# A transformer block in fp32: V by Strassen products kept in DRAM, and part of the softmax's work moved from VectorE to GpSimd

## The chip, the cores and the metric

The kernel runs on one core of a Trainium2 chip. The metric is the device time of one execution in microseconds (us). Five engines matter: PE (TensorE, matrix products into PSUM), DVE (VectorE), ACT (ScalarE), POOL (GpSimd) and SP (SyncE, whose queue issues all the DMAs here). Each engine runs its own instructions in order and waits on semaphores for what others produce.

## The reference

```
x = x + layernorm(attention(layernorm(x)))
x = x + layernorm(ffn(layernorm(x)))

attention(h):                      # h is [2, 512, 512]: 2 batches of 512 tokens
    q = rms_norm(h @ Wq + bq, gq)  # Wq, Wk, Wv: [512, 4096]; the norm is over all 4096
    k = rms_norm(h @ Wk + bk, gk)
    v = h @ Wv + bv
    split q, k, v into 32 heads of 128
    attn = softmax(q @ k.T / sqrt(128)) ; out = attn @ v, heads side by side
    return out @ Wo + bo           # Wo: [4096, 512]
ffn(x): x @ W_base.T + b_base + a small gated mixture of 8 rank-16 experts
```

All is fp32. In the trace a matmul of a 128x128 by a 128x512 tile is two PE records.

## The kernel before, in words

Everything is laid in tiles of 128 partitions by 512 fp32 (256 KB). `norm_transposed` (L132) gives the normed input transposed: for each batch four tiles `nT` of 128 features by 512 tokens.

**Projections of q and k** (`project`, L173). For each of 8 groups of 4 heads a block of weights (1 MB) is loaded, and q, then k, is made by Strassen's scheme in Winograd's form over 2x2 blocks: the two halves of the features, two halves of the group's heads, and the two batches. `token_sums` (L150) forms the four sums `t1` to `t4` of the token side once, on DVE; `weight_sums` (L162) the four of the weights for each group, on GpSimd. A group is seven products of two tiles each; ACT and DVE combine them out of PSUM. `keep_it` (L204) stores each finished head to DRAM (`keptq`, `keptk`), squares it on ACT, and adds the square to `accq` or `acck` on GpSimd (L213), for the rms norms: `rqs` (for q, one value per token in every row) and `rks` (for k, one per token in a column).

**The head loop** (L434) has 64 turns, one for each head and batch (i = 2h + b). A turn's instructions are issued in the order written, since the scheduler is told to keep the order on PE, DVE, ACT and POOL (L575):

- `fetch(i+3)`: DMAs of k and q of one head back from DRAM; `scaled(i+2)` (L323): q times the gain `gqk` and times `rqs`, on DVE.
- `sums(i)` (L345): three adds on DVE, `d`, of the four exponential tiles of turn i.
- `scores(i+1)` (L329): four products `pss`, copied by ACT with the factor `rks` into a wide tile `s` of 128x2048; the maximum of the four parts on DVE (`m`), and over partitions on GpSimd with `partition_all_reduce` (`top`, L342).
- `outward`: products `psy` of a finished group's heads with Wo, added to `ys` on DVE (`y`, L405), and `values` (L304): products `psv` of V for a later group, plain products of four feature tiles, copied by ACT into SBUF.
- `turned(i)` (L354): a 32x32-block transpose `dT` and a reduction `part` on DVE, the column sums of `d`.
- `exponentials(i+1)` (L374): the maximum subtracted from all of `s` on DVE (L376), the exponential on ACT (L377).
- `weighted(i)`: four products `o` of V with the exponentials; `reciprocals(i)`: `psd` on PE spreads the sums, then `inv` and `r` on DVE; `divided(i)`: `oh` = `o` times `r` on DVE and the bias of V on ACT.

V of a group is made during the loop, one or two tiles a turn, as tables written out by hand say (`v_tasks`, `o_tasks`, L410 to L423). After the loop come the last group's `psy`, the residual, the second norm and the FFN.

Of the kernel before, what the change touches and what calls it, by code (L numbers as in the profile page):

```python
# [15 lines left out]
P = 128  # L16
# [15 lines left out]
def kernel(ctx: ExitStack, tc: tile.TileContext, x, wq, wk, wv, wo, vecs, rows, wbase, gates, bexp, out):  # L32
# [7 lines left out]


    nc = tc.nc
    B = x.shape[0]
# [7 lines left out]
    kpool = ctx.enter_context(tc.tile_pool(name="kpool", bufs=5))  # L51
    opool = ctx.enter_context(tc.tile_pool(name="opool", bufs=GH * B + 10))
    spool = ctx.enter_context(tc.tile_pool(name="spool", bufs=3))
# [9 lines left out]
    def wide(name):  # L63
        return spool.tile([P, NT, 512], F32, tag="wide", name=name)
# [38 lines left out]
    nbthr = const.tile([P, 1], F32, tag="nbthr", name="nbthr")  # L103
    gate_sb = const.tile([P, NK, E * R + E + 1], F32, tag="gate", name="gate_sb")
    nc.sync.dma_start(out=gate_sb, in_=gates.rearrange("(c p) f -> p c f", p=P))
    bexp_sb = const.tile([P, D], F32, tag="bexp", name="bexp_sb")
    nc.sync.dma_start(out=bexp_sb, in_=bexp)

# [41 lines left out]
    def token_sums(xTs):  # L150

        (b11, b21), (b12, b22) = ((xT[0:2], xT[2:4]) for xT in xTs)
        first, second = wide("t12"), wide("t34")
        t1, t2, t3, t4 = first[:, 0:2], first[:, 2:4], second[:, 0:2], second[:, 2:4]
        for c in range(2):
            nc.vector.tensor_tensor(t1[:, c], b12[c], b11[c], ALU.subtract)
            nc.vector.tensor_tensor(t2[:, c], b22[c], t1[:, c], ALU.subtract)  # L157
            nc.vector.tensor_tensor(t3[:, c], b22[c], b12[c], ALU.subtract)
            nc.vector.tensor_tensor(t4[:, c], b21[c], t2[:, c], ALU.subtract)
        return [[t[:, c] for c in range(2)] for t in (t1, t2, t3, t4)]  # L160

# [10 lines left out]

    def project(xTs, sums, w_src, bias, step, name, pool, keep, accs, w):  # L173

# [8 lines left out]
        for g in range(G):  # L183
# [20 lines left out]
            def keep_it(o, b, j):  # L204
                h = g * GH + j
                nc.sync.dma_start(out=keep[b, h], in_=o)
                if b not in begun:
                    begun.add(b)
                    nc.scalar.activation(accs[b], o, AF.Square)
                else:  # L210
                    sq = tt(f"sq_{name}{b}_{h}")
                    nc.scalar.activation(sq, o, AF.Square)  # L212
                    nc.gpsimd.tensor_tensor(accs[b], accs[b], sq, ALU.add)  # L213

            two = range(2)
# [39 lines left out]
    def attention():  # L255
# [12 lines left out]
        keptk = dram.tile([B, H, P, 512], F32, tag="k", name="keptk")  # L268
        accq = [xpool.tile([P, 512], F32, tag="x", name=f"accq{b}") for b in range(B)]
        acck = [xpool.tile([P, 512], F32, tag="x", name=f"acck{b}") for b in range(B)]  # L270

# [4 lines left out]
        sums4 = []  # L276
        for _ in project(xTs, sums4, wq, bq, steps[:, 0, :], "q", qpool, keptq, accq, wq0):
            pass
# [15 lines left out]

        vs, wvs, wos = {}, {}, {}

        def load_wv(g):
            if g < H // GH:
                wvs[g] = load_w(wv[:, ts(g, GH * P)], f"wv{g}")

        def load_wo(g):
            wos[g] = load_w(wo[ts(g, GH * P), :], f"wo{g}")

        def values(g, n):  # L304
            b, t = divmod(n, NT)
            ps = pt(f"psv{b}_{g}_{t}")
            for c in range(NK):
                nc.tensor.matmul(ps, xTs[b][c][:, ts(t, P)], wvs[g][:, c, :], start=(c == 0), stop=(c == NK - 1))  # L308
            v = vpool.tile([P, 512], F32, tag="v", name=f"v{b}_{g}_{t}")
            nc.scalar.copy(v, ps)  # L310
            vs[b, g, t] = v

# [10 lines left out]
        def scaled(i):  # L323
            h, b = divmod(i, B)
            nc.vector.scalar_tensor_tensor(qs[i], qs[i], gqk[:, h : h + 1], rqs[b], ALU.mult, ALU.mult)

        ss, ms = {}, {}

        def scores(i):  # L329

            h, b = divmod(i, B)
            s = wide(f"s{b}_{h}")
            for k in range(NT):
                ps = pt(f"pss{b}_{h}_{k}")
                nc.tensor.matmul(ps, kk[i][:, ts(k, P)], qs[i], start=True, stop=True)  # L335
                nc.scalar.activation(s[:, k, :], ps, AF.Copy, scale=rks[b][:, k : k + 1])  # L336
            m = tt(f"m{b}_{h}")
            nc.vector.tensor_tensor(m, s[:, 0, :], s[:, 1, :], ALU.max)
            nc.vector.tensor_tensor(m, m, s[:, 2, :], ALU.max)
            nc.vector.tensor_tensor(m, m, s[:, 3, :], ALU.max)  # L340
            top = tt(f"top{b}_{h}")
            nc.gpsimd.partition_all_reduce(top, m, P, ReduceOp.max)  # L342
            ss[i], ms[i] = s, top

        def sums(i):  # L345

            s = ss[i]
            d = tt(f"d{i}")
            nc.vector.tensor_tensor(d, s[:, 0, :], s[:, 1, :], ALU.add)
            nc.vector.tensor_tensor(d, d, s[:, 2, :], ALU.add)  # L350
            nc.vector.tensor_tensor(d, d, s[:, 3, :], ALU.add)
            return d
# [9 lines left out]
        def reciprocals(i, part):  # L362

            psd = pt(f"psd{i}")
            nc.tensor.matmul(psd[:, 0:16], same.rearrange("p i c -> p (i c)"), part, start=True, stop=True)  # L365
            inv = small.tile([P, 16], F32, tag="inv", name=f"inv{i}")
            nc.vector.reciprocal(inv, psd[:, 0:16])  # L367
            r = tt(f"r{i}")
            nc.vector.transpose(
                r.rearrange("p (j c) -> p j c", c=32), inv.unsqueeze(2).to_broadcast([P, 16, 32])  # L370
            )
            return r

        def exponentials(i):  # L374
            s, top = ss[i], ms[i]
            nc.vector.tensor_tensor(s, s, top.unsqueeze(1).to_broadcast([P, NT, 512]), ALU.subtract)  # L376
            nc.scalar.activation(s, s, AF.Exp)  # L377

        os = {}

        def weighted(i):
            h, b = divmod(i, B)
            g, j = divmod(h, GH)
            po = pt(f"o{b}_{h}")
            for k in range(NT):
# [12 lines left out]
        def outward(g, n, tag=None):  # L398

            b, t = divmod(n, NT)  # L400
            ps = pt(f"psy{b}_{g}_{t}", tag)
            for j in range(GH):
# [5 lines left out]
        NG = H // GH  # L408

        v_tasks = {i: [] for i in range(N)}  # L410
        for k in range(NT):
            v_tasks[k // 2].append((0, NT + k))
        for k in range(G):
            v_tasks[2 + k * 6 // G].append((1, k))
        for i in range(G, N - G):
            v_tasks[i].append((i // G + 1, i % G))
        o_tasks = {i: [] for i in range(N)}
        early = G * (NG - 2) * 7 // 8
        for k in range(G * (NG - 1)):
            i = G + k * 8 // 7 if k < early else N - G + (k - early) * G // (G * (NG - 1) - early)  # L420
            o_tasks[i].append((k // G, k % G))
        load_wv(0)
        load_wv(1)  # L423
        for i in range(3):
            fetch(i)
        for i in range(2):
            scaled(i)
        for n in range(NT):
            if n >= 2:
                key_scales(n - 2)  # L430
            values(0, n)
        scores(0)
        exponentials(0)
        for i in range(N):  # L434
            g, n = divmod(i, G)
            if i + 3 < N:
                fetch(i + 3)
            if i + 2 < N:
                scaled(i + 2)
            if n == 4:  # L440
                load_wo(g)
                load_wv(g + 2)
            d = sums(i)
            if i + 1 < N:
                scores(i + 1)
            adds = [outward(*task) for task in o_tasks[i]]
            for task in v_tasks[i]:
                values(*task)
            part = turned(i, d)
            if i + 1 < N:  # L450
                exponentials(i + 1)
            for add in adds:
                add()
            po = weighted(i)
            divided(i, po, reciprocals(i, part))
        again = [[kpool.tile([P, 512], F32, tag="k", name=f"xr{b}_{t}") for t in range(NT)] for b in range(B)]
        for b in range(B):
            for t in range(NT):
                nc.sync.dma_start(out=again[b][t], in_=x[b, ts(t, P), :])
        wb = load_w(wbase, "wb")  # L460
        adds = [outward(NG - 1, n, "ps") for n in range(NT)]
        for add in adds:
            add()
        adds = [outward(NG - 1, NT + n, "aux") for n in range(NT)]
        for b in range(B):
# [3 lines left out]
            if b == 0:  # L469
                first = ffn(0, x2, wb)  # L470
                next(first)
# [3 lines left out]
            else:  # L475
                second = ffn(1, x2, wb)

# [22 lines left out]

    def ffn(b, xs, w):

        xT = norm_transposed(xs, f"f{b}", "ps" if b == 0 else "aux")
        yield
        hs = tmp.tile([P, NT, E * R + E + 1], F32, tag="hs", name=f"hs{b}", bufs=1)
        for t in range(NT):
# [106 lines left out]
```

## Time and profile before

| | |
|---|---|
| time, median of 3 runs (lowest to highest) | 1386.77 us (1384.13 to 1387.21) |
| time of the profiled execution | 1385.63 us |
| its span | 1383.9 us |
| mean granted clock of PE | 0.991 |
| busy: PE, DVE, ACT, POOL | 1342.4, 907.3, 503.7, 351.0 us |
| q and k projections | 15.9 to 417.8 us |
| head loop, with the first tiles of V ahead | 417.9 to 1286.6 us |
| last group's `psy`, residual, FFN | 1286.6 to 1383.9 us |

The page has numbered parts: busy times; the span in 40 slices; DMA queues; the chain of work that ended last; the costliest groups of instructions. A group's line gives the source line, engine, operation, output and inputs and the count; then the busy time and the mean ns of one; then the idle time of its engine just before, and what ended that ("releaser"; "issue" means nothing that the profile shows). A timeline line gives the start, the duration, the engine, line and operation, and the idle time before it in brackets. A line of the table of stretches gives start and end, the length, then for PE, weight load (PEld), DVE, ACT and POOL the busy time and the number of instructions, then PE's granted clock, the DMA engines' busy share and GB/s.

### The profile page before, as it was taken

What the parts mean: (1) busy time and instruction counts of PE and PEld (TensorE: products, weight loads), DVE (VectorE), ACT (ScalarE), POOL (GpSimd) and SP (SyncE); (2) the same over time, 40 slices, a digit from 0 to 9 for tenths busy, and PEclk for the clock granted to TensorE, in tenths of its full rate; (3) what the DMA queues carried; (4) which work ended last, traced back from release to release, by engine and by line L of the source; (5) the groups of instructions that cost most, each with busy time, mean ns of one, the idle gap of its engine ahead of it and who ended that gap; (6) DMA issues with size and microseconds to landing.
All of it is one profiled execution on the core that took longest, in us unless ns stands there. A gap on an engine that the chain in (4) does not pass through costs nothing.

```text
span 1383.9 us, 10495 instructions
## 1 busy us (share of the span) xinstructions
PE 1342.4 (97%) x3308; PEld 610.3 (44%) x3308; DVE 907.3 (66%) x1350; ACT 503.7 (36%) x703; POOL 351.0 (25%) x262
## 2 busy tenths in 40 slices
PE   4999999999999999999999999999999999999976
PEld 2444444444444444444444444444444444444443
DVE  6443434534343888778778777777777777887556
ACT  4122222322224444344434344343434343443333
POOL 3357556565731111111111111111111111111000
PEclk9999999999999999999999999999999999999998
DMA  6243344434333112103112111211111111200001
GB/s 231 91 150 124 117 149 144 161 106 152 122 118 118 61 46 76 46 31 107 40 37 76 61 46 61 67 40 64 58 61 42 65 48 59 76 23 16 23 1 61
DMA packets 58759, 109.84 MB, mean 79 GB/s; under 512 B 5072, under 2 KB 5712, under 8 KB 58704
## 3 DMA queue, kind: packets, MB, share of 16 engines
q1 hardware_dynamic: 58704, 109.17, 23.2%
q8 instruction: 26, 0.43, 0.1%
q14 instruction: 29, 0.24, 0.1%
HBM read 73.50 MB, written 35.65 MB: 79 GB/s over the span
## 4 chain that ended last, share of the span: by engine, by line
PE 95%; DVE 3%; ACT 1%; issue 1%; POOL 0%; DVEq 0%; POOLq 0%; ACTq 0%
PE pss L335 16%; PE psy L404 16%; PE o L386 16%; PE psv L308 15%; PE p_k L192 14%; PE p_q L192 14%; PE f L517 2%; PE f L567 1%; PE psd L365 1%; PE hg L509 1%; DVE same L264 0%; PE nt_f L139 0%; PE nt_a L139 0%; DVE nT_a L144 0%; ACT n_a L137 0%
## 5 line engine op out<-in xcount | busy, mean ns | idle before, releaser
L342 POOL PARTITION_ALL_REDUCE top<-m x64 | 114.1, 1783 | 738.7 <-DVE m L340 738.7
L335 PE MATMUL pss<-qh,kh 128*128 128x512 f32 x512 | 235.2, 602 | 0.0
L386 PE MATMUL o<-s,v 128*128 128x512 f32 x512 | 230.2, 592 | 0.0
L308 PE MATMUL psv<-wv,nT_a 128*128 128x512 f32 x512 | 229.5, 592 | 0.0
L404 PE MATMUL psy<-wo,oh 128*128 128x512 f32 x512 | 228.2, 592 | 0.0
L376 DVE TENSOR_TENSOR s<-s,top 128x2048 f32<-128x2048 f32 x64 | 146.7, 2292 | 42.5 <-POOL top L342 42.5
L377 ACT ACTIVATE s<-s 128x2048 f32<-128x2048 f32 x64 | 122.2, 1910 | 89.4 <-DVE s L376 88.4
L336 ACT ACTIVATE s<-pss,rk 128x512 f32<-128x512 f32 x256 | 154.0, 680 | 0.8 <-PE pss L335 0.8
L386 PEld LDWEIGHTS o<-s,v 128*128 128x128 f32 x512 | 97.3, 190 | 122.5 <-issue 122.2
L308 PEld LDWEIGHTS psv<-wv,nT_a 128*128 128x128 f32 x512 | 97.1, 190 | 121.5 <-issue 121.0
L404 PEld LDWEIGHTS psy<-wo,oh 128*128 128x128 f32 x512 | 97.1, 190 | 121.5 <-issue 121.0
L310 ACT COPY v<-psv 128x512 f32<-128x512 f32 x64 | 37.4, 586 | 275.8 <-PE psv L308 275.8
L335 PEld LDWEIGHTS pss<-qh,kh 128*128 128x128 f32 x512 | 92.5, 190 | 92.8 <-issue 92.8
L213 POOL TENSOR_TENSOR accq<-accq,sq_q 128x512 f32<-128x512 f32 x62 | 78.6, 1268 | 95.0 <-ACT sq_q L212 94.5
L393 ACT ACTIVATE oh<-oh,vec 128x512 f32<-128x512 f32 x64 | 46.0, 719 | 144.0 <-DVE oh L392 144.0
L213 POOL TENSOR_TENSOR acck<-acck,sq_k 128x512 f32<-128x512 f32 x62 | 78.6, 1267 | 75.4 <-ACT sq_k L212 75.0
L367 DVE RECIPROCAL inv<-psd 128x16 f32<-128x16 f32 x64 | 16.4, 256 | 118.4 <-PE psd L365 118.4
L192 PE MATMUL p_q<-t,s_q 128*128 128x512 f32 x192 | 88.0, 608 | 3.6 <-DVE t L157 3.6
L212 ACT ACTIVATE sq_q<-q 128x512 f32<-128x512 f32 x62 | 39.1, 630 | 134.3 <-DVE q L240 79.2
L212 ACT ACTIVATE sq_k<-k 128x512 f32<-128x512 f32 x62 | 39.1, 631 | 127.9 <-DVE k L240 71.4
L192 PE MATMUL p_k<-t,s_k 128*128 128x512 f32 x192 | 85.0, 592 | 0.0
L192 PEld LDWEIGHTS p_q<-t,s_q 128*128 128x128 f32 x192 | 37.3, 195 | 51.3 <-issue 48.8
(146 smaller groups left out, 1440.2 us busy)
## 6 DMA issues: line engine op xcount, KB each, us to landing
keptq<-q SPq DMA_DIRECT2D x64, 256.0 KB, 2.5
qh<-keptq SPq DMA_DIRECT2D x64, 256.0 KB, 2.9
keptk<-k SPq DMA_DIRECT2D x64, 256.0 KB, 2.4
kh<-keptk SPq DMA_DIRECT2D x64, 256.0 KB, 2.6
w_q<-in_wq SPq DMA_DIRECT2D x8, 1024.0 KB, 6.9
w_k<-in_wk SPq DMA_DIRECT2D x8, 1024.0 KB, 5.6
wv<-in_wv SPq DMA_DIRECT2D x8, 1024.0 KB, 5.6
wo<-in_wo SPq DMA_DIRECT2D x8, 1024.0 KB, 5.0
```

Of the source, the lines that this page charges most:

```text
L192: nc.tensor.matmul(ps, a[:, c, ts(j, P)], x[c], start=(c == 0), stop=(c == 1))
L212: nc.scalar.activation(sq, o, AF.Square)
L213: nc.gpsimd.tensor_tensor(accs[b], accs[b], sq, ALU.add)
L308: nc.tensor.matmul(ps, xTs[b][c][:, ts(t, P)], wvs[g][:, c, :], start=(c == 0), stop=(c == NK - 1))
L335: nc.tensor.matmul(ps, kk[i][:, ts(k, P)], qs[i], start=True, stop=True)
L336: nc.scalar.activation(s[:, k, :], ps, AF.Copy, scale=rks[b][:, k : k + 1])
L342: nc.gpsimd.partition_all_reduce(top, m, P, ReduceOp.max)
L376: nc.vector.tensor_tensor(s, s, top.unsqueeze(1).to_broadcast([P, NT, 512]), ALU.subtract)
L377: nc.scalar.activation(s, s, AF.Exp)
L386: nc.tensor.matmul(po, vs[b, g, k][:, ts(j, P)], ss[i][:, k, :], start=(k == 0), stop=(k == NT - 1))
L393: nc.scalar.activation(o, o, AF.Identity, bias=bv[:, h : h + 1], scale=1.0)
L404: nc.tensor.matmul(ps, o[:, ts(t, P)], wos[g][:, j, :], start=(j == 0), stop=(j == GH - 1))
```

## The change

- **V.** All of V is made by the same scheme of seven products for two groups at a time (`values`, now a generator of 56 steps of two tiles, with `value_weights` for the sums of the weights on GpSimd). The results go through SBUF to DRAM (`keptv`), and `fetch_v` reads a group's tiles back when the loop nears it. 42 steps stand ahead of the loop, 14 are spread over its first eight turns; the bias of V stays where it was. The token sums stay alive until then, each in a tile of its own.
- **q.** The gain `gqk` is applied to each head of q on ACT before it is stored (the square is taken first, so the norm sees q without it). In the loop `scaled` then only multiplies by `rqs`, on GpSimd.
- **Softmax.** The three adds of `sums` go to GpSimd. The subtraction of the maximum gets a function of its own, `below_top`. In turn i: `below_top(i)`, `scores(i+1)`, the exponential of i, `outward`, the transpose and reduction of i-1, the products `o` of i, the division of i-1, the sums of i.
- `outward` has one task a turn, one group behind; `pss` and `psd` take PSUM tiles of one kind, `psy` and `o` of the other.
- The expert and gate weights of the FFN are loaded at the end of the loop instead of at the start; `accq` and `acck` have buffers of their own; the pool of `o` has 16 instead of 18.

```diff
-    opool = ctx.enter_context(tc.tile_pool(name="opool", bufs=GH * B + 10))
+    opool = ctx.enter_context(tc.tile_pool(name="opool", bufs=GH * B + 8))
...
             def keep_it(o, b, j):
                 h = g * GH + j
-                nc.sync.dma_start(out=keep[b, h], in_=o)
...
+                if gain is not None:
+                    nc.scalar.activation(o, o, AF.Copy, scale=gain[:, h : h + 1])
+                nc.sync.dma_start(out=keep[b, h], in_=o)
...
+        def value_weights(p):
+
+            wa, wb = (load_w(wv[:, ts(2 * p + i, GH * P)], f"wv{2 * p + i}") for i in range(2))
+            a11, a12, a21, a22 = ([w[:, i + c, :] for c in range(2)] for w in (wa, wb) for i in (0, 2))
...
+            for c in range(2):
+                nc.gpsimd.tensor_tensor(s1[c], a21[c], a22[c], ALU.add)
+                nc.gpsimd.tensor_tensor(s2[c], s1[c], a11[c], ALU.subtract)
+                nc.gpsimd.tensor_tensor(s3[c], a11[c], a21[c], ALU.subtract)
+                nc.gpsimd.tensor_tensor(s4[c], a12[c], s2[c], ALU.subtract)
...
+                    for t in tiles:
+                        ps = product(1, a11, b11, t)
+                        u1[t] = tile_of("u1", t)
+                        nc.scalar.copy(u1[t], ps)
+                    yield
+                    for t in tiles:
+                        keep(0, 0, t, product(2, a12, b21, t), u1[t])
+                    yield
...
+        def fetch_v(b, g):
+            for t in range(NT):
+                v = vpool.tile([P, 512], F32, tag="v", name=f"v{b}_{g}_{t}")
+                nc.sync.dma_start(out=v, in_=keptv[b, g, t])
+                vs[b, g, t] = v
...
         def scaled(i):
             h, b = divmod(i, B)
-            nc.vector.scalar_tensor_tensor(qs[i], qs[i], gqk[:, h : h + 1], rqs[b], ALU.mult, ALU.mult)
+            nc.gpsimd.tensor_tensor(qs[i], qs[i], rqs[b], ALU.mult)
...
-            nc.vector.tensor_tensor(d, s[:, 0, :], s[:, 1, :], ALU.add)
-            nc.vector.tensor_tensor(d, d, s[:, 2, :], ALU.add)
-            nc.vector.tensor_tensor(d, d, s[:, 3, :], ALU.add)
+            nc.gpsimd.tensor_tensor(d, s[:, 0, :], s[:, 1, :], ALU.add)
+            nc.gpsimd.tensor_tensor(d, d, s[:, 2, :], ALU.add)
+            nc.gpsimd.tensor_tensor(d, d, s[:, 3, :], ALU.add)
...
-        def exponentials(i):
+        def below_top(i):
             s, top = ss[i], ms[i]
             nc.vector.tensor_tensor(s, s, top.unsqueeze(1).to_broadcast([P, NT, 512]), ALU.subtract)
-            nc.scalar.activation(s, s, AF.Exp)
+
+        def exponentials(i):
+            nc.scalar.activation(ss[i], ss[i], AF.Exp)
...
             if i + 2 < N:
                 scaled(i + 2)
...
-            d = sums(i)
+            below_top(i)
             if i + 1 < N:
                 scores(i + 1)
-            adds = [outward(*task) for task in o_tasks[i]]
-            for task in v_tasks[i]:
-                values(*task)
-            part = turned(i, d)
-            if i + 1 < N:
-                exponentials(i + 1)
+            exponentials(i)
+            for _ in range(14 * (i + 1) // G - 14 * i // G if i < G else 0):
+                next(v_steps)
+            adds = [outward(g - 1, n)] if g > 0 else []
+            part = turned(i - 1, d) if i > 0 else None
             for add in adds:
                 add()
-            po = weighted(i)
-            divided(i, po, reciprocals(i, part))
+            last, po = po, weighted(i)
+            if i > 0:
+                divided(i - 1, last, reciprocals(i - 1, part))
+            d = sums(i)
+        divided(N - 1, po, reciprocals(N - 1, turned(N - 1, d)))
```

## The prediction

> **What bounds the kernel now.** I read the page's busy shares first, then the chain of waits, then the costliest groups, then single stretches of time.
>
> ```profile
> PE 1342.4 (97%) x3308; PEld 610.3 (44%) x3308; DVE 907.3 (66%) x1350; ACT 503.7 (36%) x703; POOL 351.0 (25%) x262
> PE 95%; DVE 3%; ACT 1%; issue 1%; POOL 0%; DVEq 0%; POOLq 0%; ACTq 0%
> L342 POOL PARTITION_ALL_REDUCE top<-m x64 | 114.1, 1783 | 738.7 <-DVE m L340 738.7
> L308 PE MATMUL psv<-wv,nT_a 128*128 128x512 f32 x512 | 229.5, 592 | 0.0
> L213 POOL TENSOR_TENSOR accq<-accq,sq_q 128x512 f32<-128x512 f32 x62 | 78.6, 1268 | 95.0 <-ACT sq_q L212 94.5
> ```
>
> PE is the bound, in all stages: 97% busy, 95% of the chain. POOL's adds (1.27 us) belong to the q and k stages; in the head loop it has only `top` (1.78 us). One turn of the loop, from `o` to the next `o`, as the table of stretches has it:
>
> ```profile
> 912.86:926.82 13.96, 13.96 (x36) 6.30 (x35) 10.49 (x15) 5.52 (x7) 1.78 (x1) 1.00 0.12 38
> ```
>
> PE fills the turn of 13.96 us. Without `psv` a turn is 10.53 us: the chain's `pss` at 958.45 and 968.98 show one. POOL is busy 1.78 us of the 13.96. Last, POOL's start and DVE beside it, from the timeline:
>
> ```profile
> 0.86 0.20 POOL L91 MEMSET ones<- 128x128 f32 x1
> 9.08 0.28 POOL masks.py:199 TENSOR_SCALAR_AFFINE_SELECT ident<-ident 128x128 f32<-128x128 f32 x1 [8.02 <-issue]
> ...
> 12.56 1.27 POOL L167 TENSOR_TENSOR s_q<-w_q 128x512 f32<-128x512 f32 x1 [3.08 <-DMA w_q<-in_wq]
> 13.91 1.27 POOL L168 TENSOR_TENSOR s_q<-s_q,w_q 128x512 f32<-128x512 f32 x1
> 15.13 1.27 POOL L169 TENSOR_TENSOR s_q<-w_q 128x512 f32<-128x512 f32 x1
> ```
>
> ```profile
> 12.10 0.16 DVE L117 SCALAR_TENSOR_TENSOR shift_a<-mv_a,rs_a 128x1 f32<-128x1 f32 x1
> ...
> 12.57 1.27 DVE L117 SCALAR_TENSOR_TENSOR shift_a<-mv_a,rs_a 128x1 f32<-128x1 f32 x1
> ```
>
> The 8.02 us before `ident` wait for nothing that the profile shows. The order of POOL's instructions in the built program has a row without a tile exactly there: a reload of GpSimd's library (index 0). The kernel before has two reloads: this one, and one (index 1) ahead of its first `top`, hidden in a wait of 17.6 us.
>
> **What the Trainium skill says.** "GPSIMD Engine Reference", 2.1 Instruction dispatch: the first call to a freshly loaded kernel pays about 6 us (5.95 measured) "with no visible profile instruction". The trace agrees in kind: 8.02 us, nothing recorded, here beside a DMA share of 0.80. "SBUF — State Buffer", Who interferes with whom: a VectorE instruction with two SBUF inputs and a GpSimd one that reads SBUF exclude each other for the whole instruction. The trace agrees: `shift_a` takes 0.16 us alone and 1.27 beside `s_q`. "TensorE: Matmul & The Clock Gate", Part 1, halves PE's clock after idle windows of about 3.4 us; no stretch quoted here shows that.
>
> **The change on GpSimd.** This decides. The order of the changed program shows POOL's queue in a turn of the loop as: reload (library 1), `top`(i+1), reload (library 0), three adds of `d`(i), the scaling of q(i+3), and again. `partition_all_reduce` and `tensor_tensor` stand in different libraries, so each turn pays two reloads, 129 in all where there were 2. Durations: `top` 1.78. An add that needs the add before it starts 1.35 us after it (12.56 to 13.91), an independent one 1.22 (13.91 to 15.13), so three adds and the scaling take 1.35 + 1.35 + 1.23 + 1.27 = 5.20. A reload lies between 5.95 (the skill) and 8.02 (the trace, beside the opening loads at 265 GB/s). The loop moves 38 GB/s in the turn above, so I stay nearer the lower end: 6.5, an estimate. It may be less if a library is small, or more: both ends stay in the range. A turn of POOL is 2 x 6.5 + 1.78 + 5.20 = 20.0 us.
>
> Does anything hide it? The reload stands ahead of the wait of its instruction, so it would overlap that wait; but the waits are over by then. Take `top`(i) done at 0. DVE subtracts (2.29), takes the maxima of i+1 (2.3) by 4.6; ACT's exponentials (1.91) end at 4.3. POOL meanwhile reloads to 6.5, adds `d`(i-1) to 10.5, scales to 11.7, reloads to 18.2, and `top`(i+1) ends at 20.0. The maxima have waited since 4.6, the exponentials of i since 4.3: POOL never waits, all others wait for POOL. New waits: `d` for ACT, with the scaling and the next `top` queued behind (over before it is reached); `dT` on DVE for `d`, with `y`, `inv`, `r`, `oh` and the next subtraction behind: from 10.5 they need 0.70 + 0.69 + 0.68 + 0.26 + 0.71 + 0.69, some 4.2 with gaps, so done by 15, before 20.0. PE: `o` 4.3 to 7.8, then `psd` after `part` at 12, `pss` to 15.5, `psy` to 19; with gaps this long its clock may fall. At half clock throughout, its 10.53 us would be 21.1, so 1.1 us a turn at the very worst; it warms in `pss` and `psy`, so I take 0. The port exclusion costs nothing here: DVE's two-input steps fall into the reloads.
>
> **V.** PE: 224 tile products instead of 256, each two records, 64 fewer at 0.429 us (3.43 for 8): -27.4 us. ACT loses 64 copies and keeps 16; DVE gains 112 operations of 0.69 from PSUM (77 us), 14 per seven steps of 3.43 us, so 9.7 of 24 us: beside PE. POOL's 32 adds (1.27) likewise: 10.2 of 48 us. 42 of 56 steps stand before the loop. DMA: 64 stores and 64 fetches of 256 KB more on SP's queue, landing in some 2.5 us as kept k and q do; fetched one or two turns ahead: nothing. In the first eight turns two V steps (6.9 us) and 7.1 of other PE work are shorter than 20.0, so V is hidden there. **q's gain:** 64 ACT operations of about 0.7 (`oh`'s row is 719 ns) where ACT has 42 busy of 160 us in the q stage; each store of q leaves 1.3 us later, and the five buffers of q come round in about 9 us against 0.69 + 0.63 + 0.7 + 2.5 of use: nothing. Without that cover it would be 64 x 0.7 = 45 us. DVE loses `d` (3 x 0.69) and the scaling (0.76) per turn: nothing, since it doesn't bound. Fetches of gates and `bexp` move to the end behind `xr` and `wb`, needed some 30 us later: nothing.
>
> **The sum**, on the profiled execution (span 1383.9, its time 1385.63, so 1.7 outside; the median of the runs shown is 1386.77, 0.1% off). V starts at 417.9 as before. 42 steps of 3.43, `ssk` 1.6 and the first scores 3.5 bring PE to 567. The first scores lie after 39 steps, so `top`(0) ends at about 560.5. Then POOL: reload 6.5, eight adds for V's last weights 10.1, scaling 1.3, reload 6.5, `top` 1.8: `top`(1) ends at 586.7. 62 turns of 20.0, less one scaling (1.25): `top`(63) at 1825.4. Reload 6.5, `d`(62) 4.0, `d`(63) 4.0, `dT` and `part` 1.4, `psd` 0.4: 1841.7. In the kernel before, the last 64 `psy` start at 1286.6, 97.2 before the end; the tail is kept. Span 1939, time 1941.
>
> One us on the reload's price is 2 x 62 + 3 = 127 us.
>
> **The rivals.**
> 1. Reloads of 5.0 to 8.0 us, POOL bounds: 1750 to 2131, likeliest 1941. For it: the order and the 8.02. Chance 0.80.
> 2. A reload over 8 us, as at the start: at 9.0, 1941 + 2.5 x 127 = 2258. Against: light DMA in the loop. 0.06.
> 3. Reloads shorter than 5 us, as with a small library: at 3.5, 1560. Before's time is met at 6.5 - 555/127 = 2.1 us. 0.07, of which 0.01 within 0.2%.
> 4. The other side: the reload is nearly free (the 8.02 us were the queue's own start-up). It decides below about 1.9 us, where POOL's turn meets PE's 10.53. Then PE bounds, and the matmuls' 27.4 us are saved, less some 4 for the adds of the last `d`: 1362, faster. 0.04.
> 5. Free reloads, but the shared port bounds: POOL 1.78 + 5.20 and DVE 2.29 + 2.3 exclude each other, 11.6 a turn instead of 10.53; 56 turns x 1.0 on 1362: about 1420, slower. Against: `top` may not hold the port. 0.03.
>
> Range 1750 to 2131, case 1, which leaves 0.20 out. Measurement tells 0.2% from no change: faster 0.04 (case 4), same 0.01, slower 0.95.
>
> **What would show it.** `pss` comes every 20 us instead of 13.96 or 10.53. POOL sits idle some 6.5 us before each `top` and each first `d`, with "issue" as releaser, though `m` and the exponentials are long done. The chain goes over POOL and issue in the loop, not PE; PE's share falls to about 1315 of 1939, 68% (more if its clock falls). Matmuls of V: 448 records. Wrong if POOL's gaps are short, if `d` waits for ACT, or if turns are set by PE or DVE.

## The result and the profile after

The changed kernel takes 1959.0 us (median of 4 runs, 1955.95 to 1965.95); the kernel before, run beside it, 1385.88. The ratio is 1.414, with a 95% interval of [1.410, 1.419]. The forecast was 1941 us, in a range of 1750 to 2131. The profiled execution of the changed kernel took 1955.95 us, with a span of 1953.9 us and a mean granted clock of PE of 0.894.

First the page of the changed kernel: busy shares, then the chain of work that ended last (the part of it by engine).

```profile
PE 1510.7 (77%) x3244; PEld 654.8 (34%) x3244; DVE 818.5 (42%) x1206; ACT 538.3 (28%) x719; POOL 713.4 (37%) x550
...
PE 33%; issue 21%; DVE 19%; POOL 19%; ACT 6%; DMA 1%; SPq 0%; POOLq 0%; ACTq 0%; DVEq 0%
```

No engine is near full. PE, 97% busy before, is idle for 23% of the span, and POOL, which holds the others up, is busy for only 37%. So the busy shares don't name what sets the time. The costliest groups do, when they are ranked by the idle time ahead of them:

```profile
L407 POOL PARTITION_ALL_REDUCE top<-m x64 | 115.3, 1802 | 452.4 <-issue 373.0
L414 POOL TENSOR_TENSOR d<-s 128x512 f32<-128x512 f32 x64 | 80.1, 1252 | 454.6 <-issue 454.6
```

Before, `top` had 738.7 us of idle time ahead of it, and all of it was a wait for DVE's maxima. Now 373.0 us ahead of `top` and 454.6 us ahead of the first add `d` end by nothing that the profile shows: 827.6 us in all, 63 gaps each, 5.92 and 7.22 us on the average. POOL's timeline shows one turn and the start of the next:

```profile
1003.14 1.25 POOL L414 TENSOR_TENSOR d<-s 128x512 f32<-128x512 f32 x1 [6.78 <-issue]
1004.47 1.26 POOL L415 TENSOR_TENSOR d<-d,s 128x512 f32<-128x512 f32 x1
1005.82 1.26 POOL L416 TENSOR_TENSOR d<-d,s 128x512 f32<-128x512 f32 x1
1007.04 1.26 POOL L390 TENSOR_TENSOR qh<-qh,rq 128x512 f32<-128x512 f32 x1
1014.15 1.80 POOL L407 PARTITION_ALL_REDUCE top<-m  x1 [5.85 <-issue]
1024.08 1.25 POOL L414 TENSOR_TENSOR d<-s 128x512 f32<-128x512 f32 x1 [8.13 <-issue]
```

This is the predicted queue, instruction by instruction, with a silent gap at each of the two places where the built program has a reload of GpSimd's library. DVE's last maximum (L405) had ended by 1000.9, so `top` at 1014.15 waited for nothing but its own queue. The stretch of one turn, from `o` to `o`:

```profile
1000.75:1020.34 19.59, 15.98 (x27) 6.50 (x27) 7.93 (x11) 5.27 (x6) 6.80 (x5) 0.74 0.09 27
```

POOL is busy 6.80 us of 19.59; PE's granted clock is down to 0.74, and the work for which PE needs 10.53 us at full clock keeps it busy for 15.98.

A trap in this profile is the chain of waits. For the same turn it has these pieces (start, length, what):

```profile
998.78 1.92 ACT s L444
1000.70 2.44 issue
1003.14 1.26 POOL d L414
...
1010.28 0.70 DVE oh L459
1010.98 3.17 issue
1014.15 1.81 POOL top L407
```

It follows the events that an instruction's semaphores show, so it steps from `d` back to the exponential and from `top` back to `oh`, and leaves only 2.44 and 3.17 us to "issue". POOL itself stood idle for 6.78 and 5.85 us: the exponential and `oh` ran beside the reloads and held nothing up. That is why "issue" is 21% in the chain, and not 827.6 of 1953.9 = 42%.

### The profile page after: what moved, and what is told of

Read it like the earlier page. It is cut to its first block, busy times and chain, and to the rows that moved or that the text cites. A ratio compares the mean times of both kernels' runs of the same rounds, so it can differ in the third digit from the quotient of the medians.

```text
span 1953.9 us, 11254 instructions
## 1 busy us (share of the span) xinstructions
PE 1510.7 (77%) x3244; PEld 654.8 (34%) x3244; DVE 818.5 (42%) x1206; ACT 538.3 (28%) x719; POOL 713.4 (37%) x550
## 4 chain that ended last, share of the span: by engine, by line
PE 33%; issue 21%; DVE 19%; POOL 19%; ACT 6%; DMA 1%; SPq 0%; POOLq 0%; ACTq 0%; DVEq 0%
PE p_k L190 10%; PE p_q L190 10%; PE v L328 7%; DVE s L441 7%; ACT s L444 6%; POOL top L407 6%; POOL d L416 4%; POOL d L415 4%; POOL d L414 4%; DVE dT L422 2%; DVE r L434 2%; DVE part L424 2%; DVE oh L459 2%; PE psy L471 2%; PE f L582 1%
## 5 line engine op out<-in xcount | busy, mean ns | idle before, releaser
L453 PE MATMUL o<-s,v 128*128 128x512 f32 x512 | 273.7, 684 | 149.1 <-ACT s L444 148.9
L400 PE MATMUL pss<-qh,kh 128*128 128x512 f32 x512 | 349.2, 845 | 4.2 <-POOL qh L390 4.2
L407 POOL PARTITION_ALL_REDUCE top<-m x64 | 115.3, 1802 | 452.4 <-issue 373.0
L414 POOL TENSOR_TENSOR d<-s 128x512 f32<-128x512 f32 x64 | 80.1, 1252 | 454.6 <-issue 454.6
L430 PE MATMUL psd<-part,same 128*128 128x16 f32 x128 | 34.3, 346 | 247.8 <-DVE part L424 244.9
L422 DVE STREAM_TRANSPOSE dT<-d 128x512 f32<-128x512 f32 x64 | 45.5, 711 | 404.0 <-POOL d L416 404.0
L401 ACT ACTIVATE s<-pss,rk 128x512 f32<-128x512 f32 x256 | 170.5, 682 | 100.0 <-PE pss L400 99.9
L400 PEld LDWEIGHTS pss<-qh,kh 128*128 128x128 f32 x512 | 137.1, 281 | 166.0 <-issue 157.6
L430 PEld LDWEIGHTS psd<-part,same 128*128 128x128 f32 x128 | 27.6, 268 | 300.6 <-DVE part L424 300.6
L328 PE MATMUL v<-s_v,t 128*128 128x512 f32 x192 | 85.9, 594 | 1.9 <-POOL s_v L311 1.9
L415 POOL TENSOR_TENSOR d<-d,s 128x512 f32<-128x512 f32 x64 | 80.7, 1262 | 5.0
L416 POOL TENSOR_TENSOR d<-d,s 128x512 f32<-128x512 f32 x64 | 80.7, 1261 | 5.0
```

Of the source, the lines that this page charges most:

```text
L328: nc.tensor.matmul(ps, x[c][:, ts(t, P)], a[c], start=(c == 0), stop=(c == 1))
L414: nc.gpsimd.tensor_tensor(d, s[:, 0, :], s[:, 1, :], ALU.add)
L415: nc.gpsimd.tensor_tensor(d, d, s[:, 2, :], ALU.add)
L416: nc.gpsimd.tensor_tensor(d, d, s[:, 3, :], ALU.add)
L453: nc.tensor.matmul(po, vs[b, g, k][:, ts(j, P)], ss[i][:, k, :], start=(k == 0), stop=(k == NT - 1))
```

## The experiments

The theory was that two library reloads a turn set the turn. Rivals were that POOL's longer work does, or the SBUF port that POOL shares with DVE, or the new order, in which a turn's softmax is spread over three turns. "Scaling" is q's multiplication by `rqs`. The first four kernels have one time each, beside 1387.81 us for the kernel before; the others have an interval.

### Sums and scaling back on DVE

```diff
-            nc.gpsimd.tensor_tensor(qs[i], qs[i], rqs[b], ALU.mult)
+            nc.vector.tensor_tensor(qs[i], qs[i], rqs[b], ALU.mult)
...
-            nc.gpsimd.tensor_tensor(d, s[:, 0, :], s[:, 1, :], ALU.add)
+            nc.vector.tensor_tensor(d, s[:, 0, :], s[:, 1, :], ALU.add)
```

and the other two adds likewise; all else as in the changed kernel.

> The changed kernel with the three sums and q's scaling back on VectorE, at the same places in the order, so that GpSimd has only the all-reduce in the loop (4 library reloads after the first instead of 128). Theory (reloads set the turn): the GpSimd gaps of 5.9 and 7.3 us vanish. The turn is then set by the loop subtraction 2.29, exponential 1.91, o 3.44, psd, inv, r, oh about 2.0, sums and scaling 2.8 on VectorE, some 13.2 us: about 567 + 64 x 13.2 + 97 = 1510 us. Rival (softmax over three turns, the port shared by VectorE and GpSimd, or PE's lower clock cost the time): the reloads are only idle time; the time stays above 1800.

Measured: 1498.2 us. 461 us of the loss of 573 are gone with these four instructions a turn. What is left of the loss is a turn of 12.51 us, longer than PE's: DVE's steps lie back to back but for one wait, for `psd`, with `d` and the subtraction queued behind it:

```profile
1002.67 0.26 DVE L432 RECIPROCAL inv<-psd 128x16 f32<-128x16 f32 x1 [1.79 <-PE psd L430]
```

### Only the sums back on DVE

The scaling stays on POOL, one 1.26 us instruction a turn beside `top`.

> As the run before, but q's scaling stays on GpSimd: one 1.26 us multiplication a turn between two all-reduces, so all 128 reloads stay. Theory: a turn is 7.3 + 5.9 + 1.8 + 1.3 = 16.3 us, so 1959 - 62 x 3.8 = 1723 us, some 210 above the run with both on VectorE, for one instruction of 1.3 us a turn. Rival (the amount of work on GpSimd counts, 3.1 us of a turn): not slower than the run with both on VectorE.

Measured: 1717.2 us. The expectation was 1723. Against the kernel with none of the four on POOL, a single instruction of 1.26 us costs 219 us, 3.4 us a turn. POOL's timeline:

```profile
911.73 1.25 POOL L390 TENSOR_TENSOR qh<-qh,rq 128x512 f32<-128x512 f32 x1 [6.92 <-DVE y L472]
918.92 1.80 POOL L407 PARTITION_ALL_REDUCE top<-m  x1 [5.94 <-issue]
927.93 1.25 POOL L390 TENSOR_TENSOR qh<-qh,rq 128x512 f32<-128x512 f32 x1 [7.21 <-DVE y L472]
```

From scaling to scaling 16.2 us pass, of which POOL works 3.05; the pair of gaps, 5.94 and 7.21, is that of the changed kernel. The label `y` ahead of the scaling misleads: the gap starts as soon as `top` ends, and `y`'s semaphore only happens to come in it.

### No all-reduce

```diff
-            top = tt(f"top{b}_{h}")
-            nc.gpsimd.partition_all_reduce(top, m, P, ReduceOp.max)
-            ss[i], ms[i] = s, top
+            ss[i], ms[i] = s, m
```

This kernel leaves out the maximum over partitions: each partition subtracts its own. The sums and the scaling stay on POOL.

> The changed kernel with the maximum over partitions left out (each partition subtracts its own maximum, so the softmax is not the reference's); sums and scaling stay on GpSimd, no reload is left after the first. Theory: PE sets the turn of 10.53 us: about 1360 to 1380 us. Rival (GpSimd's adds are too slow, or exclude VectorE on the shared port): GpSimd's 5.2 and VectorE's 4.6 us of two-input work remain; well above 1420 us.

Measured: 1367.85 us, PE 97% busy, a turn of 10.52 us. POOL does more work per turn than `top` is long, and holds nothing up:

```profile
911.90 1.27 POOL L412 TENSOR_TENSOR d<-s 128x512 f32<-128x512 f32 x1 [5.34 <-ACT s L442]
```

Its gap is now a wait for the exponentials, and no "issue" is left in the loop. So neither the adds on POOL nor the order over three turns cost the 573 us; the mixture of the two kinds does. When PE bounds, the change without its reloads and without the maximum is about 20 us faster than the kernel before (1387.81 to 1367.85, one run each); this kernel doesn't separate what V, q's gain and the rest have in it.

### The kernel before, with a tiny add

```diff
             nc.gpsimd.partition_all_reduce(top, m, P, ReduceOp.max)
+            tiny = small.tile([P, 1], F32, tag="tiny", name=f"tiny{b}_{h}")
+            nc.gpsimd.tensor_tensor(tiny, epst[:, 0:1], epst[:, 1:2], ALU.add)
```

> The kernel before with one 128x1 add on GpSimd after each all-reduce, whose result nobody reads. Theory: each turn now pays two reloads, 7.3 + 5.9 + 1.8 + 0.2 = 15.2 us on GpSimd against 13.4 us a turn on average on PE: about 1386 + 64 x 1.8 = 1500 us. Rival (a reload is free and the gaps have another cause in the changed kernel): 1386 to 1393 us.

Measured: 1528.94 us, 141 us more than the kernel before, for 64 additions of one element per partition:

```profile
909.61 0.51 POOL L344 TENSOR_TENSOR tiny<-epst 128x1 f32<-128x1 f32 x1 [6.82 <-issue]
916.36 1.80 POOL L342 PARTITION_ALL_REDUCE top<-m  x1 [6.24 <-issue]
924.96 0.53 POOL L344 TENSOR_TENSOR tiny<-epst 128x1 f32<-128x1 f32 x1 [6.79 <-issue]
```

The turn shown is 15.4 us, against 13.96 of PE's work. So the price is there without anything else that the change does. The mean gaps are 458.5 / 64 = 7.2 us ahead of `tiny` and 391.8 / 63 = 6.2 ahead of `top`; with them the turn is a little over the 15.2 us that were expected, and the time 29 us over the expected 1500.

The gaps ahead of `top` aren't all alike. The longest and one of the shortest, as stretches of the table:

```profile
973.09:981.27 8.18, 8.18 (x22) 3.77 (x21) 3.24 (x5) 0.88 (x2) 0.00 (x0) 1.00 0.40 128
1366.78:1372.52 5.74, 4.39 (x12) 1.85 (x11) 3.95 (x6) 1.00 (x2) 0.01 (x2) 1.00 0.00 0
```

In the first the DMA engines were 40% busy, in the second idle. Of all 63, the 51 gaps with a DMA share under 5% have a mean of 5.98 us, the 11 with over 30% one of 7.36 (in the kernel with only the sums back on DVE: 5.90 and 6.57). The prediction went below the 8.02 us of the start since the loop moves less data; this agrees with it, though no run changed the DMAs alone.

### Sums on DVE, early in the turn

From the first experiment (sums and scaling on DVE): `sums(i-1)` is moved right ahead of `turned(i-1)`, and the scaling behind the scores, to take DVE's wait for `psd` away.

```diff
             if i + 1 < N:
                 scores(i + 1)
+            if i + 2 < N:
+                scaled(i + 2)
...
-            part = turned(i - 1, d) if i > 0 else None
+            part = turned(i - 1, sums(i - 1)) if i > 0 else None
...
-            d = sums(i)
```

> All elementwise work back on VectorE as in the first run, but ordered behind the maxima: the sums of turn i-1 right before their transpose, q's scaling after the scores, so that neither stands between oh and the next subtraction. Theory: the first run's 12.5 us a turn came from that order (1.79 us of VectorE waiting for psd in each turn); now VectorE's own 10.7 us or PE's 10.5 set the turn: 1498 - 62 x 1.75 = 1390 us, about the kernel before. Rival (the exponential spread over three turns is late anyway, whatever the order): 1450 or more.

Measured: 1447.23 us, ratio 1.0437 [1.0421, 1.0452]. The wait is gone, but the turn is 11.59 us, and the expectation missed by 57 us. The cause stands in two lines, DVE's first add and the all-reduce beside it:

```profile
1011.38 2.08 POOL L407 PARTITION_ALL_REDUCE top<-m  x1 [9.52 <-DVE m L405]
1011.74 1.53 DVE L414 TENSOR_TENSOR d<-s 128x512 f32<-128x512 f32 x1
```

The add takes 1.53 us instead of 0.68, `top` 2.08 instead of 1.78. DVE has no gap in this turn, so the 0.85 us are all but the whole excess of 11.59 over the expected 10.7. This looks like the shared port, which the prediction priced at nothing, since there DVE's two-input steps fell into reloads. Here an add lies beside the all-reduce in every turn; a later experiment moves it away.

### q scaled ahead of the loop

From the last kernel: the scaling goes back to POOL, but out of the loop, into the k and V stages ahead of it, where no all-reduce runs. Each head of q is read back, scaled, and stored in `scaledq`, which `fetch` then reads.

```diff
+                    nc.sync.dma_start(out=q, in_=keptq[b, h])
...
+                    nc.gpsimd.tensor_tensor(q, q, rqs[(i - 1) % B], ALU.mult)
...
+                    nc.sync.dma_start(out=scaledq[b, h], in_=tiles.pop(i - 2))
...
-            nc.sync.dma_start(out=q, in_=keptq[b, h])
+            nc.sync.dma_start(out=q, in_=scaledq[b, h])
```

> As the run before, but q is scaled once ahead of the loop: during the k and V stages GpSimd multiplies each kept head of q (1.27 us) and it is stored again, so GpSimd does elementwise work only while its library for that is loaded, and VectorE has 10.1 us a turn in the loop. 32 MB more of DMA over some 250 us. Theory: PE sets every turn (10.5 us), as in the run without the all-reduce: 1365 to 1372 us, some 1.2% faster than before, with the maximum kept. Rival (the extra DMAs delay the stores and weights of the k and V stages, or VectorE is still late): 1385 or more.

Measured: 1408.73 us, ratio 1.0157 [1.0143, 1.0171]; missed too. The turn is 10.87 us and DVE's, which has no gap in it. With the scaling gone, the all-reduce falls on the second add (L450, 1.41 us; `top` 2.08 again). Of the first eight turns from `o` to `o`, where V's steps stand too, five take 15.1 us or more.

### Starting with the right library loaded

At the start of the kernel before, `ident` waits 8.02 us; in the changed kernel 0.29. The two end with different libraries: the all-reduce's, or that of the elementwise operations. One tiny add behind the head loop of the kernel before changes what it ends with, and so what its next execution starts with.

```diff
             divided(i, po, reciprocals(i, part))
+        tiny = small.tile([P, 1], F32, tag="tiny", name="tiny")
+        nc.gpsimd.tensor_tensor(tiny, epst[:, 0:1], epst[:, 1:2], ALU.add)
```

> The kernel before with a single 128x1 add on GpSimd after the last all-reduce, whose result nobody reads. It leaves the elementwise library loaded at the end. Theory of residence (a reload of the library that is already there is nearly free, and the 8 us at the start are paid because the execution before left the other one): the idle time before ident falls from 8.0 to 0.3 us, PE's first product of q comes some 4 us earlier, and the time falls by 2 to 4 us, to about 1383. Rival (the 8 us are the start-up of GpSimd's queue): no change at the start, 1386.

Measured: 1384.48 us, ratio 0.9986 [0.9979, 0.9993]. The gain of 1.9 us is just under the 2 to 4 that were expected, and the gap at the start is gone:

```profile
1.35 0.30 POOL masks.py:199 TENSOR_SCALAR_AFFINE_SELECT ident<-ident 128x128 f32<-128x128 f32 x1 [0.29 <-POOL ones L91]
```

The reading that fits all traces of this case: the library outlives the execution, and a reload of the one that is there is all but free. The same line added to the kernel with q scaled ahead gained nothing in time:

> q scaled ahead, with the single 128x1 add at the end as well. Theory: both gains add up: 2 to 4 us below the run with q scaled ahead, about 1364, some 1.5% faster than before.

Measured: 1408.81 us, ratio 1.0158 [1.0143, 1.0172], as without the line. The gap is 0.29 us, and PE's first product of q starts 4.8 us earlier (at 12.67 instead of 17.46). But PE then waits 8.63 us instead of 3.72 for the second batch's normed input, and by the second group of q only 0.4 us is left (56.31 against 56.73). In the kernel before, 2.4 of 3.4 us were left there (53.23 against 55.64). Why so little is left here stays open.

### Sums behind y

From the kernel with q scaled ahead: `sums(i)` goes behind `y` and ahead of `inv`, so `dT`, `part` and `y` lie beside `top`. The work is the same; the sums made in turn i are now those of turn i, and not those of the turn before.

```diff
-            part = turned(i - 1, sums(i - 1)) if i > 0 else None
+            part = turned(i - 1, d) if i > 0 else None
             for add in adds:
                 add()
+            d = sums(i)
```

> The kernel with q scaled ahead, but a turn's sums of exponentials go on the vector engine behind y, ahead of inv, so that its two-input additions lie behind the all-reduce and its one-input steps (dT, the row sum, y) lie beside it. Theory (the all-reduce holds the port that two-input operations need, which made the additions 1.41 us and the all-reduce 2.08 us, and with them the turn 10.87 us): the additions go back to about 0.68 us, the all-reduce to 1.80, the vector engine needs about 10.1 us a turn, the matrix engine's 10.53 us bound the turn, and the first eight turns no longer take 15.1 us; about 1375 to 1385 us, the stall at the start of the loop staying. Rival (the vector engine's own work, or the order over three turns, bounds, not the port): 1405 us or more, turn 10.8 us.

Measured: 1383.36 us, ratio 0.9979 [0.9971, 0.9987]. With nothing but the place changed, 25 us are gone. DVE's timeline, of the part of a turn that lay beside and behind `top` (1000.11 to 1001.89):

```profile
999.86 0.70 DVE L457 STREAM_TRANSPOSE dT<-d 128x512 f32<-128x512 f32 x1
1000.60 0.69 DVE L459 TENSOR_REDUCE part<-dT 128x16 f32<-128x512 f32 x1
1001.20 0.68 DVE L507 TENSOR_TENSOR y<-psy,y 128x512 f32<-128x512 f32 x1
1001.80 0.68 DVE L449 TENSOR_TENSOR d<-s 128x512 f32<-128x512 f32 x1
...
1004.34 0.26 DVE L467 RECIPROCAL inv<-psd 128x16 f32<-128x16 f32 x1 [0.41 <-PE psd L465]
```

Every add takes 0.68 to 0.69 us, `top` 1.78, and DVE waits again, so PE sets the turn of 10.52 us. Turns with two of V's steps take 14.3 us instead of 15.1. `y` has two inputs as well, one of them in PSUM, and isn't stretched. So the overlap of two-input adds with the all-reduce made the turns too long in the two misses; the rival, DVE's own work, is out. That what they hold against each other is the port is the Trainium skill's reading (cited at the end); the runs show who stretches whom.

### One reload at the start of the loop

In the kernel just shown, the gathering of V's last weight sums stands between two all-reduces, which makes a pair of reloads; PE waited 6.67 us for the exponentials there. The first scores are moved behind the gathering.

```diff
-            if n == steps_of_v - kept_back - 4:
+            if n == steps_of_v - kept_back - 1:
                 scores(0)
```

> The kernel before this one in the list (sums behind y), with the scores of the first turn made one step ahead of the end of V's steps in place of four, so that the gathering of V's last row sums comes ahead of the first all-reduce and only one change of GpSimd's library lies at the start of the loop in place of three. Theory: the stall of about 5 us ahead of the loop goes and the time is 1366 to 1372 us, under both kernels. Rival (the stall comes from the order of the scores and V's products, not from the reloads): within 3 us of the kernel with sums behind y, or slower.

Measured: 1376.61 us, ratio 0.9938 [0.9926, 0.9950]: below the kernel before, though 5 us above the expected band. PE's wait at the start of the loop is 2.19 us instead of 6.67. In the table of stretches PE fills a turn:

```profile
1000.43:1010.95 10.52, 10.52 (x28) 4.71 (x27) 9.73 (x15) 4.83 (x6) 1.78 (x1) 1.00 0.47 136
```

PE's busy time is 19.9 us less than before (1322.5 against 1342.4), its idle time 10.4 us more. The waits say where:

```profile
PE o L488 <- ACT s L479: 4.8, 3, 2.5
PE p_q L190 <- DVE t L155: 3.6, 2, 2.2
PE v L367 <- POOL s_v L350: 3.5, 1, 3.5
PE psd L465 <- DVE part L459: 3.2, 1, 3.2
```

`o` and `v` waited for nothing in the kernel before, and `psd` for 1.0 us: some 10.5 us at the two ends of the V stage and at the end of the loop.

### The scaling in the loop, on DVE

From the kernel just shown, q isn't scaled ahead; one more DVE operation a turn stands behind the sums.

```diff
+            if i + 2 < N:
+                scaled(i + 2)
```

> As the one-reload kernel, but q is not scaled ahead: its scaling is one more two-input operation of the vector engine in each turn, behind the sums. Theory: the vector engine then has about 10.1 + 0.65 = 10.75 us a turn against the matrix engine's 10.53, so it bounds by a little: 1378 to 1388 us, 13 us or so above the one-reload kernel. Rival (the port and the reloads were all that stood against the vector engine, and it still hides): within 3 us of the one-reload kernel.

Measured: 1394.17 us, ratio 1.0055 [1.0043, 1.0068]. The sign is the theory's, the size 6 us over its band. Turns of 10.63 us, in which DVE has no wait, alternate with turns of 10.87, in which it waits 0.16 us for `psd`; and most of the turns with V's steps are about 1 us longer (15.3 against 14.3), which the expectation had left out. The work of DVE in a turn is that of the kernel with the sums early in the turn, whose turn was 11.59 us: with the adds behind the all-reduce it is 0.7 to 1.0 us shorter.

## Why the prediction was right

**The mechanism holds.** Two reloads a turn were predicted from the order of the built program, from one unexplained 8.02 us gap, and from the Trainium skill ("GPSIMD Engine Reference", 2.1 Instruction dispatch). Each of its signs is there: the gaps by "issue", `pss` every 20 us, 448 records of V's products. Without the all-reduce the whole loss is gone, without the four elementwise instructions 461 of 573 us, and one tiny add a turn makes a loss of 141 us in the kernel before.

**The price of a reload (6.5 us) was right as a mean and wrong as one number.** The two aren't alike: 5.92 us for the all-reduce's library, 7.22 for the elementwise one, 6.57 on the average. The skill's 5.95 fits the first alone. The estimate was put between two figures by judgement; that it fell on the mean of two different prices was luck, and it made the time come out within 1%. The turn of POOL is then 5.92 + 1.80 + 7.22 + 5.14 = 20.08, and measured 20.07 against the forecast's 20.0. From the end of `top`(1) to that of `top`(63) 1244.6 us passed against 1238.75, and the last reload added 0.5: 6.3 of the 15.0 us by which the forecast span of 1939 was short.

**The start of the loop: 6.3 us missed.** `top`(1) was to end at 586.7 and ended at 593.03. `top`(0) ended 2.5 us later than forecast, the gap ahead of V's weight sums was 9.43 us, not 6.5, and the first four of these adds took 1.53 to 1.72 us instead of 1.26, some 1.5 us together, against 0.5 us won on the second reload. What ended the gap of 9.43 us isn't settled. The longer adds are the port exclusion, which the prediction took as nothing: DVE's three maxima, each with two inputs in SBUF, lay beside these four adds, and took 1.57 to 1.76 us instead of 0.69. One of each:

```profile
572.79 1.76 DVE L403 TENSOR_TENSOR m<-s 128x512 f32<-128x512 f32 x1
574.08 1.60 POOL L311 TENSOR_TENSOR s_v<-s_v,wv 128x512 f32<-128x512 f32 x1
```

The next add on POOL, behind the last of these maxima, took 1.25 us again. Inside the turns the term was rightly nothing: the subtraction took 2.29 us before and after.

**PE's clock: right for the turn, not for the tail.** It did fall, to 0.74 in the turn shown. The forecast had it rise again in `pss` and `psy`; but the records of `pss` grew from 602 to 845 ns, and only those of `psy` were near their old length (596 against 592). It cost nothing within a turn, since PE's part was over before POOL released the next: 15.98 of 19.59 us. From the last 64 `psy` to the end, though, 99.5 us passed instead of 97.2, with PE busy for 79.86 us instead of 77.52 at a clock of 0.89 instead of 0.93: the remaining 2.3. PE's share of 77% instead of 68% is this too: longer records, not more work.

**V, and q's gain.** V's products took 229.5 us before and 202.3 after in the one-reload kernel: 27.2 against the predicted 27.4. From the first product of q's second group to that of k's first 168.23 us passed before and after, so q's gain cost nothing. That the rest of V's work is hidden is shown only for the kernels in which PE bounds: there about 10 us of new waits of PE stand against it.

**The other side** (a nearly free reload, 1362 us) had the 8.02 us as the queue's own start-up. That is refuted: the gap is 0.29 us when the library is there already. Its figure for a loop without reloads was near: 1367.85 without the all-reduce. (By the prediction's own sum POOL's turn meets PE's 10.53 us at a reload of 1.8 us, not 1.9: a slip without weight.) The rival by the port was not the cause here, but its doubt, that `top` may not hold the port, was wrong: in two of the repairs the all-reduce and DVE's adds stretched each other.

## What to carry to other kernels

Before an operation is moved to a half-empty engine, look at what else is in that engine's queue: here 5.14 us of work fitted easily into 12 us of idle time, and brought 13.1 us of reloads with it, because it was of another library than its neighbour. Keep one kind of GpSimd operation in a loop, and do the other kind ahead of it. On DVE, place one-input steps, or those that read one input from PSUM, beside the all-reduce, and the steps with two inputs in SBUF behind it: the place alone was worth 25 us.

## What the hardware showed beyond that

- A reload of a library that is already there is all but free (0.29 us), and what is loaded stays from one execution to the next: the idle time ahead of `ident` was 7.86 to 9.4 us in the eight programs whose last GpSimd operation is an all-reduce, and at most 0.29 in the five that end with an elementwise one. In the kernel before this was worth 1.9 us.
- The two directions differ: 5.9 us to the all-reduce's library, 7.2 to the elementwise one, in the changed kernel; 6.2 and 7.2 in the kernel before with a tiny add, where the gaps ahead of the all-reduce beside busy DMA engines were the longer ones (7.36 us against 5.98).
- An all-reduce over partitions and a DVE operation with two inputs in SBUF hold each other up: 0.68 us became 1.41 to 1.53, and the all-reduce's 1.78 became 2.08. The Trainium skill ("SBUF — State Buffer", Who interferes with whom) says that such DVE instructions contend with GpSimd ones that read SBUF, and that the shared pair of ports is an exclusive lock. These runs agree that they contend. They don't show a lock for the whole of the all-reduce: one after the other the two would take 1.78 + 0.68 = 2.46 us, and both were over in 2.08.
